# RWKV6 block in a fused hybrid layer: token differences made by TensorE, a second product for the decay's token, three mixing buffers, and a moved order of norms, copies and own terms

## The chip, the core and the metric

The kernel runs on one NeuronCore of a Trainium2 chip. The metric is the device time of one execution in microseconds, taken as the median of several executions. The profile is one further execution, seen by the hardware profiler. Its engines are PE (TensorE, matrix products), PEld (TensorE's weight loads), DVE (VectorE), ACT (ScalarE), POOL (GpSimd) and SP (SyncE, which here only starts transfers).

## The reference

The input `x` has 4 sequences of 1024 tokens with 256 channels, all in float32. Four sublayers are added to it one after another, each on a layer-normalised copy: a retention attention, a mixture of experts (8 experts, the best 2 for each token), an RWKV6 attention, and the same mixture of experts again. The change concerns the RWKV6 part:

```python
def _rwkv6_forward(x, time_maa_x, time_maa_wkvrg, tm_w1, tm_w2, time_decay, td_w1, td_w2, time_faaaa, Wr, Wk, Wv, Wg, Wo, ln_w, ln_b):
    Bb, Tt, Cc = x.shape
    sx = jnp.concatenate([jnp.zeros_like(x[:, :1]), x[:, :-1]], axis=1) - x
    xxx = x + sx * time_maa_x
    m = jnp.tanh(xxx @ tm_w1).reshape(Bb, Tt, 5, A)
    delta = jnp.einsum('btfa,fac->btfc', m, tm_w2)
    mix = time_maa_wkvrg[None, None] + delta
    xw, xk, xv, xr, xg = [x + sx * mix[:, :, i] for i in range(5)]
    r = xr @ Wr
    k = xk @ Wk
    v = xv @ Wv
    g = jax.nn.silu(xg @ Wg)
    ww = time_decay + jnp.tanh(xw @ td_w1) @ td_w2
    w = jnp.exp(-jnp.exp(ww))
    ...
    def step(state, rkvw):
        r_t, k_t, v_t, w_t = rkvw
        a = k_t[..., :, None] * v_t[..., None, :]
        y = jnp.einsum('bhk,bhkv->bhv', r_t, state + u[None, :, :, None] * a)
        new_state = w_t[..., :, None] * state + a
        return (new_state, y)
    ...
    yn = (y - mu) * jax.lax.rsqrt(var + EPS)
    yn = yn * ln_w.reshape(H, K) + ln_b.reshape(H, K)
    return yn.reshape(Bb, Tt, Cc) * g @ Wo
```

There are 16 heads of 16 channels (H, K), A is 32 and the decay's inner width is 64. `sx` is the difference between the token before and the token itself; the five mixed tokens `xw`, `xk`, `xv`, `xr`, `xg` are called mixing 0 to 4 below.

## The kernel before

**Stages.** The retention attention fills the first 285 us or so of the profiled execution. Two expert stages follow, for the two halves of the tokens; during the second one, the first block of the RWKV6 part is prepared in between (`prepare`, lists `first`). The RWKV6 stage runs from about 684 to 1303 us, and two more expert stages end the kernel. In the expert stages, tiles of 128 gathered tokens go through `fetch`, `up`, `turn` and `down`; `down` writes its result to a buffer `m_y` (L719, four buffers), which GpSimd scatters to DRAM (L720).

**The RWKV6 stage.** The tokens are cut into 8 blocks of 512 tokens, two per sequence; the loop at the end of `hybrid_kernel` goes over the blocks j and over 8 steps n in each. A step makes two `run` calls (h = 0 and 1), so that 16 calls cover the states of a block. One `run` multiplies v, broadcast from DRAM into `w_vb`, by k (L984, VectorE), scans it along time with the decay (L986, two scans) into `w_s`, and multiplies the states by r (L994, GpSimd). TensorE then adds the products over channels into `w_yp` (`sums`, L1017), one step later. `w_wk` holds the decay factor and k for one half of the channels (`factors`, L926 and L927, ScalarE); its two buffers are written once each per block.

**Beside the scans** each step does a part of the work for the next block j+1 and the rest of the work for the block before. The order of both is written out by hand: the tables `amid` (after the first `run` of a step), `late` (after the second), `uses` (small VectorE operations between two scans of a `run`) and `given` (which mixing products are made after which `run`). Each entry names the block relative to j. The engines TensorE, ScalarE, VectorE, GpSimd and, in this stage, the transfer queue of SyncE take their instructions strictly in the order in which these tables issue them.

**From tokens to the mixed tokens.** `normed` takes the statistics of a block (VectorE, then four small GpSimd operations), normalises into `w_xn` (L809, ScalarE, tokens on partitions) and puts the last column of the block before at the head of `w_xT`. `turn` transposes to `w_xT` (L212, L213; channels on partitions, 513 columns) and makes `w_sx`, the difference of neighbouring columns, on GpSimd (L825). `mix` makes the inner products of the token mix (L837, L840). `deltas` makes the five mixing products (L854), adds the constant part on ScalarE (L866), multiplies by `w_sx` (L867) and adds the token (L868), both on GpSimd; in blocks 6 and 7 mixings 0 and 2 take one VectorE operation (L864) in place of L866 and L867. The results lie in `w_xf`, four buffers. `decay` and `decay2` (L876, L887) make the decay from mixing 0, `projected` (L898) makes v, k, r and g from the others.

**From the states to the output.** The own term of a token is r times k (`paired`, L909, `w_rk`), summed over channels by TensorE (`own`, L915, `w_cp`) and multiplied by v (`bonus`, L920). `centre`, `spread`, `root`, `spread_out` and `gated` are the normalisation over heads; `out_part` (L220) is the output projection in two parts (0 and 2), and `added` puts them onto the residual (L225).

**PSUM.** Nearly all products share three buffers of one bank (`psum`, tag `mm`), so a product waits until the reader of an older one is done.

Of the kernel before, what the change touches and what calls it, by code (L numbers as in the profile page):

```python
# [42 lines left out]
P = 128  # L43
# [31 lines left out]
N_KEEP = O_PAD + NSL  # L75
# [28 lines left out]
def hybrid_kernel(  # L104
# [71 lines left out]
    dest = cst[:, O_DEST : O_DEST + HT]  # L176
    empty = cst[:, O_PAD : O_PAD + NSL]
# [287 lines left out]
    class Half:  # L465
# [245 lines left out]
        def down(self, j):  # L711
            op = psum([P, C], "m_op", "yp")
            for c in range(KC):
                mm(op, lhsT=self.aT[j][:, c, :],  # L714
                   rhs=w2a[:, bass.ds(self.ev[j], 1), c, :].rearrange("p o n -> p (o n)"),
                   start=(c == 0), stop=(c == KC - 1))
            g, i = divmod(j, GRP)
            y = px.tile([P, C], F32, name="m_y", tag="m_y", bufs=4)
            nc.scalar.activation(y, op, AF.Copy, scale=self.share[g][:, i : i + 1])  # L719
            nc.gpsimd.indirect_dma_start(  # L720
                out=y_views[self.half][j][:, :],
                out_offset=bass.IndirectOffsetOnAxis(ap=self.to[g][:, i : i + 1], axis=0),
                in_=y, in_offset=None,
            )
# [61 lines left out]
    def rwkv(pi, w):  # L786
# [13 lines left out]

        def normed(j):
            d = st[j]
            r = res[j]
            rstd = small.tile([P, NT], F32, name="w_rstd", tag="rstd")
            shift = small.tile([P, NT], F32, name="w_shift", tag="shift")
            stats_of(r, rstd, shift, "w_")
# [10 lines left out]
        def turn(j):  # L817
            d = st[j]
            xT = d["xT"]
            for n in range(2):  # L820
                across(lambda i: d["xn"][:, i, :], n,
                       xT[:, :, 1 + 2 * n * P : 1 + (2 * n + 2) * P], "w_")
            d["now"] = xT[:, :, 1 : BLK + 1]
            d["sx"] = full(pi, "w_sx", 1)
            nc.gpsimd.tensor_sub(d["sx"], xT[:, :, 0:BLK], d["now"])  # L825
# [18 lines left out]
        def deltas(j, parts):  # L844
# [12 lines left out]
            def mixed():  # L857
                for f, c, dp in dps:
                    if c == 0:
                        d["xf", f] = full(pi, "w_xf", 4)  # L860
# [7 lines left out]
                    nc.gpsimd.tensor_add(xf, xf, d["now"][:, c, :])  # L868
# [3 lines left out]
        def decay(j):  # L872
            d = st[j]
            tp = psum([P, BLK], "w_twp")
            for c in range(KC):
                mm(tp[:64, :], lhsT=w["td_w1"][:, c, :], rhs=d["xf", 0][:, c, :],  # L876
                   start=(c == 0), stop=(c == KC - 1))
# [197 lines left out]
        def out_part(j, i):  # L1075
            st[j]["op"] = project_part(st[j]["z"], w["o"], i, "w_")

        def added(j, i):
            add_part(st[j]["op"], res[j], i)

        def both(j, parts):
# [6 lines left out]
            [(0, normed)],  # L1088
            [(0, turn)],
# [3 lines left out]
            [(0, both, [(2, 0), (2, 1)]), (0, decay), (1, normed)],  # L1093
# [4 lines left out]
            [(1, turn)],  # L1098
# [12 lines left out]
            0: [(0, factors, 1), (1, mix, 0)],  # L1111
            1: [(0, own, 0), (0, projected, "g", 4)],
# [3 lines left out]
            5: [(1, decay2), (2, normed)],  # L1116
            6: [(1, projected, "k", 1)],
            7: [(-1, out_part, 2), (1, projected, "r", 3), (1, factors, 0)],
        }
        late = {  # L1120
            0: [],
            1: [(-1, centre, 1), (0, own, 1)],
# [4 lines left out]
            6: [(-1, out_part, 0)],  # L1127
            7: [(2, turn), (0, centre, 0)],
# [3 lines left out]
            (1, 0): [(0, paired, 1)],  # L1132
            (1, 1): [(0, bonus, 0)],
# [61 lines left out]
        def finish(n):  # L1195

            if n == 0:
                sums(NBLK - 1, 7)
# [5 lines left out]
    def rwkv_inputs(pi):  # L1204
# [17 lines left out]
        for n, src in (("v", w_v), ("g", w_g)):  # L1222
            t = pi.tile([P, KC, C], F32, name=f"w_{n}")
            flat = pi.tile([P, KC, C], F32, name=f"w_{n}0", tag="w_xf", bufs=4)
# [277 lines left out]
def constants():  # L1502
# [9 lines left out]
    c[:, O_NUM : O_NUM + NSL] = np.arange(NSL)  # L1512
    c[:, O_DEST : O_DEST + HT] = P * np.arange(HT) + i[:, None]
# [74 lines left out]
```

## Time and profile before

| | us |
|---|---|
| median of the shown runs | 1632.54 (1630.13 to 1636.39, 3 runs) |
| the profiled execution, own time | 1625.96 |
| its span | 1623.7 |
| busy PE, DVE, ACT, POOL | 1389.8, 989.4, 617.1, 937.0 |
| mean granted TensorE clock | 0.907 |

Of the RWKV6 stage alone, 684 to 1303 us: PE 504.6, DVE 553.0, ACT 243.1, POOL 544.6 us busy, clock 0.85. In the page's part 2 each digit is the busy share of a fortieth of the span in tenths. In a table of windows each row is a stretch of time with the busy time of every engine and, at the end, the granted TensorE clock as a share of full speed. In a row of groups stand the line, the engine, the operation, output and inputs, the count, the busy time, the mean duration in ns, and after the second bar the idle time of the engine before these instructions with what ended it. In a row of waits stand who waited for whom, the time in all, how often, and the longest. In a timeline row stand start, duration, engine, line, what is done, and in brackets the idle time before with its releaser. A float32 product shows as two records.

### The profile page before, as it was taken

To read this page: it belongs to the slowest core of one execution; us is meant where nothing else is said; L and a number is where in the kernel's file an instruction comes from. 1 tells how busy PE (TensorE), PEld (TensorE's weight loads), DVE (VectorE), ACT (ScalarE), POOL (GpSimd) and SP (SyncE) were. 2 spreads that over 40 slices of the span, in tenths; PEclk is the share of its full clock that TensorE was granted. 3 is DMA by queue.
4 is the path that set the end of the run, shared out by engine and by line. 5 is a ranking of instruction groups with operands and counts; after the bars stand their busy time and mean duration, and the time that the engine had idled before them with its cause. 6 is when DMAs were issued, how large, how long until landed. Compare 5 with 4: busy or idle time off the path is not lost.

```text
span 1623.7 us, 21398 instructions
## 1 busy us (share of the span) xinstructions
PE 1389.8 (86%) x6812; PEld 730.0 (45%) x6812; DVE 989.4 (61%) x1866; ACT 617.1 (38%) x1474; POOL 937.0 (58%) x895
## 2 busy tenths in 40 slices
PE   6999998868988899988879888897697679989993
PEld 4666665645555554522233333332232235555662
DVE  6566655423423532397979798989989824323534
ACT  2333434323443333444343444352344133443331
POOL 4233323723365345299999899976699832553331
PEclk9999998979999999998989799987788578999997
DMA  8931211232234431266655454533355921334625
GB/s 299 324 111 45 61 53 43 78 105 83 92 112 132 130 102 56 63 161 157 161 130 155 104 150 110 151 96 91 107 144 148 271 90 47 117 113 146 200 82 178
DMA packets 111595, 202.82 MB, mean 125 GB/s; under 512 B 12192, under 2 KB 73600, under 8 KB 111488
## 3 DMA queue, kind: packets, MB, share of 16 engines
q1 hardware_dynamic: 89280, 153.47, 33.1%
q0 software_dynamic: 17856, 41.70, 8.3%
q10 hardware_dynamic: 4352, 6.29, 1.3%
q8 instruction: 59, 0.97, 0.3%
q14 instruction: 48, 0.39, 0.1%
HBM read 140.96 MB, written 60.45 MB: 124 GB/s over the span
## 4 chain that ended last, share of the span: by engine, by line
PE 55%; POOL 18%; DVE 11%; issue 6%; ACT 6%; DMA 2%; another core or an unknown queue 0%; SPq 0%; ACTq 0%; POOLq 0%; DVEq 0%
PE m_hp L680 15%; POOL w_s L994 8%; PE m_op L714 7%; PE a_qkp L286 3%; PE w_pp L898 3%; DVE w_s L986 3%; POOL w_xf L867 3%; POOL w_xf L868 2%; PE a_yp L345 2%; PE m_xtp L671 2%; PE m_atp L707 2%; PE a_sp L325 2%; PE w_yp L1017 2%; PE w_dp L854 2%; PE a_op L220 2%
## 5 line engine op out<-in xcount | busy, mean ns | idle before, releaser
L720 POOL DMA_INDIRECT y_all<-m_y,m_to x156 | 150.9, 967 | 309.6 <-ACT m_xt L675 179.2
L994 POOL TENSOR_TENSOR w_s<-w_s,w_rT 128x1024 f32<-128x1024 f32 x128 | 304.1, 2417 | 34.0 <-DVE w_s L986 27.8
L680 PE MATMUL m_hp<-w1a,m_xt 128*128 x624 | 309.4, 620 | 12.5 <-ACT m_xt L675 12.3
L686 DVE TENSOR_TENSOR m_a<-m_hp,m_sg 128x256 f32<-128x256 f32 x156 | 66.1, 424 | 344.4 <-ACT m_sg L684 300.7
L714 PE MATMUL m_op<-w2a,m_aT 128*128 x624 | 165.1, 388 | 15.1 <-ACT m_y L719 10.8
L984 DVE TENSOR_TENSOR w_vb<-w_vb,w_wk 128x1024 f32<-128x1024 f32 x128 | 153.2, 1197 | 31.4 <-ACT w_wk L927 28.2
L986 DVE TENSOR_TENSOR_SCAN w_s<-w_wk,w_carry,w_vb 128x512 f32<-128x512 f32 x128 | 160.9, 1276 | 9.9 <-PE w_yp L1017 2.2
L986 DVE TENSOR_TENSOR_SCAN w_s<-w_wk,w_vb 128x512 f32<-128x512 f32 x128 | 152.7, 1215 | 15.4 <-ACT w_carry L1004 7.3
L680 PEld LDWEIGHTS m_hp<-w1a,m_xt 128*128 128x128 f32 x624 | 111.6, 199 | 94.4 <-issue 80.4
L652 POOL DMA_INDIRECT xg_all<-m_row,m_at x128 | 124.6, 973 | 45.9 <-issue 30.0
L1017 PE MATMUL w_yp<-w_s,core_c 128*32 128x512 f32 x512 | 104.8, 708 | 42.6 <-POOL w_s L994 32.0
L684 ACT ACTIVATE m_sg<-m_hp 128x256 f32<-128x256 f32 x156 | 60.1, 385 | 172.7 <-PE m_hp L680 141.0
L719 ACT ACTIVATE m_y<-m_op,m_share 128x256 f32<-128x256 f32 x156 | 74.0, 474 | 133.5 <-PE m_op L714 90.0
L714 PEld LDWEIGHTS m_op<-w2a,m_aT 128*128 128x128 f32 x624 | 107.5, 192 | 30.2 <-ACT m_y L719 17.0
L298 POOL TENSOR_TENSOR a_t<-a_t,a_t 128x512 f32<-128x512 f32 x32 | 41.1, 1285 | 119.1 <-DVE a_t L297 108.9
L867 POOL TENSOR_TENSOR w_xf<-w_xf,w_sx 128x512 f32<-128x512 f32 x72 | 94.0, 1306 | 24.1 <-ACT w_xf L866 23.0
L868 POOL TENSOR_TENSOR w_xf<-w_xf,w_xT 128x512 f32<-128x512 f32 x80 | 87.1, 1091 | 5.7
L707 PEld LDWEIGHTS m_atp<-cst,m_a 128*128 128x128 f32 x312 | 43.9, 144 | 93.7 <-issue 75.3
L328 DVE TENSOR_TENSOR a_pt<-a_sp,ret_c 128x2048 f32<-128x2048 f32 x32 | 73.1, 2285 | 15.8 <-PE a_sp L325 15.7
L675 ACT COPY m_xt<-m_xtp 128x256 f32<-128x256 f32 x156 | 57.1, 367 | 35.7 <-PE m_xtp L671 33.8
L671 PE MATMUL m_xtp<-cst,m_xg 128*128 128x128 f32 x312 | 62.5, 284 | 6.9 <-DMA m_xg<-xg_all 6.2
L709 DVE COPY m_aT<-m_atp 128x256 f32<-128x256 f32 x156 | 64.8, 415 | 5.4 <-PE m_xtp L671 2.6
(228 smaller groups left out, 2411.9 us busy)
## 6 DMA issues: line engine op xcount, KB each, us to landing
w_vb<-v_all SPq DMA_DIRECT2D x125, 512.0 KB
m_xg<-xg_all SPq DMA_DIRECT2D x36, 520.0 KB
tab<-in_rope SPq DMA_DIRECT2D x32, 512.0 KB
m_back<-y_all SPq DMA_DIRECT2D x48, 256.0 KB
xg_all<-zero SPq DMA_DIRECT2D x18, 520.0 KB
v_all<-w_vT SPq DMA_DIRECT2D x64, 128.0 KB
res<-in_x SPq DMA_DIRECT2D x8, 512.0 KB
w1a<-in_w SPq DMA_DIRECT2D x8, 512.0 KB
```

The costliest lines, as they stand in the source:

```text
L652: nc.gpsimd.indirect_dma_start(out=xg_views[self.half][2 * i + n][:, :], out_offset=bass.IndirectOffsetOnAxis(ap=self.at[n][:, i : i + 1], ...
L671: nc.tensor.transpose(tp[:, c, :], self.xg[j // GRP][:, j % GRP, c * P : (c + 1) * P], ident)
L680: mm(hp, lhsT=self.xt[j][:, c, :], rhs=w1a[:, bass.ds(self.ev[j], 1), c, :].rearrange("p o n -> p (o n)"), start=(c == 0), stop=(c == KC - 1))
L707: nc.tensor.transpose(tp[:, c, :], self.act[j][:, c * P : (c + 1) * P], ident)
L714: mm(op, lhsT=self.aT[j][:, c, :], rhs=w2a[:, bass.ds(self.ev[j], 1), c, :].rearrange("p o n -> p (o n)"), start=(c == 0), stop=(c == KC - 1))
L720: nc.gpsimd.indirect_dma_start(out=y_views[self.half][j][:, :], out_offset=bass.IndirectOffsetOnAxis(ap=self.to[g][:, i : i + 1], axis=0), ...
L867: nc.gpsimd.tensor_mul(xf, xf, sx)
L868: nc.gpsimd.tensor_add(xf, xf, d["now"][:, c, :])
L984: nc.vector.tensor_mul(vb, vb, wk[:, 1:2, :].to_broadcast([P, 2, BLK]))
L986: nc.vector.tensor_tensor_scan(s[:, q, 1 : BLK + 1], wk[:, 0, :], vb[:, q, :], 0.0 if j % NB == 0 else st[j - 1]["carry"][:, n, 2 * h + q ...
L994: nc.gpsimd.tensor_mul(s[:, :, 0:BLK], s[:, :, 0:BLK], d["r"][:, g, :].unsqueeze(1).to_broadcast([P, 2, BLK]),)
L1017: mm(d["yp", g][32 * q : 32 * q + 32, :], lhsT=w["sel"][:, i, :], rhs=d["s", n, q // 2][:, q % 2, 0:BLK], start=False, stop=(i == 3), skip ...
```

## The change

- The constants get a 128x128 matrix `lag` with -1 on the diagonal and +1 above it. A new function `lagged` makes `w_sx` on TensorE: for each of the four token tiles and both channel halves one product of `w_xn` with `lag`, and, but for the first tile, a one-column product that adds the last token of the tile before. ScalarE copies the result to `w_sx` in two copies. For the second block of a sequence GpSimd adds the head column of `w_xT` to the first column. The GpSimd difference in `turn` is gone.
- For mixing 0 the token is no longer added on GpSimd; `decay` makes two more products, of `td_w1` with the token itself, in the same sum.
- `w_xf` has three buffers, `m_y` six.
- `normed` is split into `norms` (statistics) and `normed` (normalisation and head column).
- In the steps: the statistics stay in step 5 and the normalisation goes to step 6; `turn` goes from step 7 to step 6, `lagged` stands at the end of step 7; output part 0 goes from late to amid in step 6, part 2 from amid in step 7 to late in step 6, each with a PSUM handle of its own; `factors` 0 of the next block goes ahead of the r projection in step 7; `centre` 0 goes from the end of step 7 to the middle of the next step 0; `own` 0 goes to the end of step 0, `own` 1 to the middle of step 1; `paired` 1 goes from step 1 to step 0 and `bonus` 0 from the second to the first `run` of step 1.

```diff
@@ hybrid_kernel, constants
+    lag = cst[:, O_LAG : O_LAG + P]
@@ Half.down
-            y = px.tile([P, C], F32, name="m_y", tag="m_y", bufs=4)
+            y = px.tile([P, C], F32, name="m_y", tag="m_y", bufs=6)
@@ rwkv
-        def normed(j):
-            d = st[j]
-            r = res[j]
+        def norms(j):
+            d = st[j]
             rstd = small.tile([P, NT], F32, name="w_rstd", tag="rstd")
             shift = small.tile([P, NT], F32, name="w_shift", tag="shift")
-            stats_of(r, rstd, shift, "w_")
+            stats_of(res[j], rstd, shift, "w_")
+            d["norm"] = rstd, shift
+
+        def normed(j):
+            d = st[j]
+            r = res[j]
+            rstd, shift = d["norm"]
             xn = d["xn"] = pi.tile([P, NT, C], F32, name="w_xn", tag="w_xn", bufs=1)
...
             d["now"] = xT[:, :, 1 : BLK + 1]
-            d["sx"] = full(pi, "w_sx", 1)
-            nc.gpsimd.tensor_sub(d["sx"], xT[:, :, 0:BLK], d["now"])
+
+        def lagged(j):
+
+            d = st[j]
+            xT = d["xT"]
+            sx = d["sx"] = full(pi, "w_sx", 1)
+            for n in range(2):
+                lp = psum([P, 2 * KC, P], "w_lp").rearrange("p (i k) t -> p i k t", k=KC)
+                for i in range(2):
+                    t = 2 * n + i
+                    for k in range(KC):
+                        cols = slice(k * P, (k + 1) * P)
+                        mm(lp[:, i, k, :], lhsT=d["xn"][:, t, cols], rhs=lag, start=True,
+                           stop=(t == 0))
+                        if t > 0:
+                            mm(lp[:, i, k, 0:1], lhsT=d["xn"][96:P, t - 1, cols],
+                               rhs=ident[96:P, P - 1 : P], start=False, stop=True)
+                nc.scalar.copy(
+                    sx[:, :, 2 * n * P : (2 * n + 2) * P].rearrange("p k (i t) -> p i k t", i=2),
+                    lp)
+            if j % NB > 0:
+                nc.gpsimd.tensor_add(sx[:, :, 0:1], sx[:, :, 0:1], xT[:, :, 0:1])
...
-                        d["xf", f] = full(pi, "w_xf", 4)
+                        d["xf", f] = full(pi, "w_xf", 3)
...
-                    nc.gpsimd.tensor_add(xf, xf, d["now"][:, c, :])
+                    if f > 0:
+                        nc.gpsimd.tensor_add(xf, xf, d["now"][:, c, :])
...
         def decay(j):
             d = st[j]
             tp = psum([P, BLK], "w_twp")
-            for c in range(KC):
-                mm(tp[:64, :], lhsT=w["td_w1"][:, c, :], rhs=d["xf", 0][:, c, :],
-                   start=(c == 0), stop=(c == KC - 1))
+            for n, z in enumerate((d["now"], d["xf", 0])):
+                for c in range(KC):
+                    mm(tp[:64, :], lhsT=w["td_w1"][:, c, :], rhs=z[:, c, :],
+                       start=(n + c == 0), stop=(n + c == KC))
...
         first = [
-            [(0, normed)],
-            [(0, turn)],
+            [(0, norms), (0, normed)],
+            [(0, turn), (0, lagged)],
...
-            [(1, turn)],
+            [(1, turn), (1, lagged)],
...
         amid = {
-            0: [(0, factors, 1), (1, mix, 0)],
-            1: [(0, own, 0), (0, projected, "g", 4)],
+            0: [(0, factors, 1), (1, mix, 0), (-1, centre, 0)],
+            1: [(0, own, 1), (0, projected, "g", 4)],
             2: [(1, mix, 1)],
             3: [(1, projected, "v", 2)],
             4: [(-1, spread_out, 0), (1, decay)],
-            5: [(1, decay2), (2, normed)],
-            6: [(1, projected, "k", 1)],
-            7: [(-1, out_part, 2), (1, projected, "r", 3), (1, factors, 0)],
+            5: [(1, decay2), (2, norms)],
+            6: [(2, normed), (1, projected, "k", 1), (-1, out_part, 0)],
+            7: [(1, factors, 0), (1, projected, "r", 3)],
         }
         late = {
-            0: [],
-            1: [(-1, centre, 1), (0, own, 1)],
+            0: [(0, own, 0)],
+            1: [(-1, centre, 1)],
             2: [(-1, spread)],
             3: [],
             4: [(-1, spread_out, 1)],
             5: [(1, store)],
-            6: [(-1, out_part, 0)],
-            7: [(2, turn), (0, centre, 0)],
+            6: [(2, turn), (-1, out_part, 2)],
+            7: [(2, lagged)],
         }
         uses = {
             (0, 0): [(0, paired, 0)],
-            (1, 0): [(0, paired, 1)],
-            (1, 1): [(0, bonus, 0)],
+            (0, 1): [(0, paired, 1)],
+            (1, 0): [(0, bonus, 0)],
             (2, 0): [(0, bonus, 1)],
...
         def finish(n):
 
             if n == 0:
+                centre(NBLK - 1, 0)
                 sums(NBLK - 1, 7)
@@ constants
+    c[:, O_LAG : O_LAG + P] = np.eye(P, k=1) - np.eye(P)
```

More of the change, by code (lines that the diff above doesn't have):

```diff
@@ L74 @@
 O_PAD = O_DEST + HT
-N_KEEP = O_PAD + NSL
+O_LAG = O_PAD + NSL
+N_KEEP = O_LAG + P
 O_CAUSAL = 0
@@ L798, in full @@
             return where.tile([P, KC, n], F32, name=name, tag=name, bufs=bufs)
+        def norms(j):
+            d = st[j]
+            rstd = small.tile([P, NT], F32, name="w_rstd", tag="rstd")
+            shift = small.tile([P, NT], F32, name="w_shift", tag="shift")
+            stats_of(res[j], rstd, shift, "w_")
+            d["norm"] = rstd, shift
         def normed(j):
@@ L803, in normed @@
             r = res[j]
-            rstd = small.tile([P, NT], F32, name="w_rstd", tag="rstd")
-            shift = small.tile([P, NT], F32, name="w_shift", tag="shift")
-            stats_of(r, rstd, shift, "w_")
+            rstd, shift = d["norm"]
             xn = d["xn"] = pi.tile([P, NT, C], F32, name="w_xn", tag="w_xn", bufs=1)
@@ L1075, in out_part @@
         def out_part(j, i):
-            st[j]["op"] = project_part(st[j]["z"], w["o"], i, "w_")
+            st[j]["op", i] = project_part(st[j]["z"], w["o"], i, "w_")
         def added(j, i):
-            add_part(st[j]["op"], res[j], i)
+            add_part(st[j]["op", i], res[j], i)
         def both(j, parts):
@@ L1092, in rwkv @@
             [(0, both, [(1, 0), (1, 1)])],
-            [(0, both, [(2, 0), (2, 1)]), (0, decay), (1, normed)],
+            [(0, both, [(2, 0), (2, 1)]), (0, decay), (1, norms), (1, normed)],
             [(0, both, [(3, 0), (3, 1)])],
@@ L1223, in rwkv_inputs @@
             t = pi.tile([P, KC, C], F32, name=f"w_{n}")
-            flat = pi.tile([P, KC, C], F32, name=f"w_{n}0", tag="w_xf", bufs=4)
+            flat = pi.tile([P, KC, C], F32, name=f"w_{n}0", tag="w_xf", bufs=3)
             nc.sync.dma_start(out=flat, in_=src.rearrange("(k p) n -> p k n", p=P))
```

## The prediction

> **What bounds the kernel now.** I read the page's 40 slices first, to see which engine is full where.
>
> ```profile
> PE   6999998868988899988879888897697679989993
> ...
> DVE  6566655423423532397979798989989824323534
> ...
> POOL 4233323723365345299999899976699832553331
> ```
>
> A slice is 40.6 us. In slices 18 to 32 VectorE and GpSimd are full together and TensorE is not: that is the RWKV stage (TensorE's own slices there are mostly 7 to 9). Before and after it lie the expert stages, where TensorE is full. The chain that ended last agrees: inside the stage it runs over GpSimd's products `w_s` (L994), the mixing products (L867, L868) and VectorE's scans (L986). So I cut the stage at each block's first `w_vb` product on VectorE; three of the eight blocks:
>
> ```profile
> core 0: us, PE busy (x) PEld busy (x) DVE busy (x) ACT busy (x) POOL busy (x), PEclk, DMA share, GB/s
> ...
> 755.50:828.50 73.00, 60.77 (x207) 21.23 (x206) 67.84 (x79) 30.10 (x66) 71.65 (x48) 0.93 0.65 155
> 828.50:907.00 78.50, 68.35 (x232) 24.91 (x232) 66.30 (x79) 32.45 (x64) 72.70 (x67) 0.87 0.57 141
> 907.00:983.00 76.00, 66.16 (x233) 24.60 (x232) 68.13 (x79) 33.16 (x72) 68.17 (x48) 0.89 0.44 122
> ```
>
> VectorE has about 68 us of work per block, GpSimd 68 to 73, and a block takes 73 to 78.5. Neither is full alone: each waits for the other, through TensorE and ScalarE. What VectorE, which drives the recurrence, waits for in the whole stage:
>
> ```profile
> DVE w_vb L984 <- ACT w_wk L927: 28.2, 7, 15.9
> DVE w_bonus L920 <- PE w_cp L915: 11.6, 7, 2.5
> DVE w_s L986 <- ACT w_carry L1004: 7.3, 2, 6.2
> ```
>
> The 15.9 us is the entry into the stage; the rest of the first row, 12.3 us, is some 2.4 us at the end of most blocks. All its waits after the entry come to 47 us (these three rows without the 15.9 give 31.2). Last, the timeline at the end of block 2 shows where they come from:
>
> ```profile
> 892.46 2.08 ACT L809 ACTIVATE w_xn<-res,w_shift,w_rstd 128x256 f32<-128x256 f32 x4 [11.78 <-POOL w_xT L813]
> ...
> 894.82 1.92 PE L1017 MATMUL w_yp<-w_s,core_c 128*32 128x512 f32 x4 [3.20 <-POOL w_s L973]
> 896.67 3.78 PE L220 MATMUL w_op<-w_o,w_sq 128*128 128x256 f32 x8
> 900.25 2.33 PE L898 MATMUL w_pp<-w_xf,w_r 128*128 128x512 f32 x4
> ...
> 907.01 1.22 DVE L984 TENSOR_TENSOR w_vb<-w_vb,w_wk 128x1024 f32<-128x1024 f32 x1 [2.58 <-ACT w_wk L927]
> ...
> 923.24 1.12 PE L915 MATMUL w_cp<-w_rk,w_sum 128*128 128x512 f32 x2
> ...
> 924.40 0.69 DVE L920 TENSOR_TENSOR w_bonus<-w_cp,w_vT 128x512 f32<-128x512 f32 x1 [1.59 <-PE w_cp L915]
> ```
>
> TensorE stands still until GpSimd delivers `w_s` (894.8), and then owes everything at once: output part 2, the r projection, mixing product 4, the turn, the centring, another sum, the token mix, and only then the own term `w_cp` (923.2). The decay factors `w_wk` queue on ScalarE behind the r copies of that chain.
>
> **The change, part by part.**
>
> GpSimd loses work. Prices:
>
> ```profile
> L868 POOL TENSOR_TENSOR w_xf<-w_xf,w_xT 128x512 f32<-128x512 f32 x72 | 78.3, 1091 | 5.0
> ...
> L825 POOL TENSOR_TENSOR w_sx<-w_xT 128x1024 f32<-128x1024 f32 x7 | 13.3, 1894 | 3.8 <-ACT w_xT L213 3.8
> ```
>
> Per block one difference (1.89) and the two additions of mixing 0 (2 x 1.09): 4.07 us, seven times 28.5 us. Added: four 2-column additions, some 0.2 us each by the 2-column copy L815 (186 ns). This is no direct gain; it lowers the lower bound of a block on GpSimd (length less its idle time over 0.25 us) from 72.7, 74.2, 69.4 to 68.6, 70.1, 65.3 in the three blocks shown, near or below VectorE's (70.4, 68.5, 70.6).
>
> TensorE gains work: per block 8 products of 128x128 and 6 one-column corner products (8 less the 2 of the first token tile), each in two passes, 28 records; and for the decay two more products, 4 records. Nearest rows: L512, also 128 weight columns with few moving columns, and L876 itself.
>
> ```profile
> 868.52 1.95 PE L512 MATMUL m_lp<-wr,m_tT 128*128 128x8 f32 x16
> ...
> 618.47 1.93 PE L876 MATMUL w_twp<-w_xf,w_td_w 128*64 128x512 f32 x4
> ```
>
> The next record begins 1.81 us after the first (0.113 each) and 1.87 us after the second. So 28 x 0.113 + 1.87 = 5.0 us per block at full clock. The Trainium skill (TensorE: Matmul & The Clock Gate, Back-to-back issue gap) gives N/2.4 + 2.5 ns, or some 25 ns for the smallest: 16 x 56 + 12 x 25 + 4 x 216 ns = 2.1 us. The row is twice that and this kernel's own float32, so I take 5.0. In the RWKV stage TensorE idles 10 to 12 us per block, which covers it; without cover it is 5 us per block. But the preparation of block 0 lies in the second expert stage, which TensorE bounds (163 of 176 us busy): there all 5.0 us count. Block 1's difference, 3.2 us, falls just after the entry, into a block with 13 us of TensorE gaps: nothing, at most 3.2.
>
> ScalarE gains two copies per block (L213's price, 0.59 each). It is 40% busy: no throughput cost. But they bring a wait: `w_sx` has one buffer, so the copy follows GpSimd's last multiplication by the old one, and TensorE's difference products, and behind it on ScalarE stand the second `w_wk` pair and so VectorE's second `w_rk`, which the change also moves ahead, from step 1 to step 0. In block 3 GpSimd ends that multiplication near 911.8, 4.8 us after VectorE began the block; two copies and the pair take 2.4 us more: 7.2. VectorE asks after two vb products, three scans and one `w_rk`, about 6.9 us.
>
> Moves. `factors` goes ahead of the r copies: the pair that ended at 906.98 can run behind the k copies, near 897, and the 2.4 us stop at block ends goes: -12.3. The statistics stay in step 5 while the four normalisations go to step 6, which gives GpSimd half a step more before ScalarE stops for it; the 6.2 us in block 0 came through such a stop (ScalarE's carry copy was late): -6.2. The own terms go ahead of a sum and of mixing products, so the old `w_cp` waits go: -11.6.
>
> What is late next is the same chain. Output parts 0 and 2 and the turn now stand before the sum, but the turn needs the normalisation, which ends 2.1 us after GpSimd's statistics (892.4 to 894.5), then two k copies and a turn copy, then output part 2 and the sum: r begins 8 to 10 us after the statistics, as now (900.25). From r to the own term, by the rows of this boundary, partly at half clock: r 5.7, mixing 4.6, difference 3.2 with 1.3 for its copy, sum 1.9, token mix 4.2, centring 1.8, own term 0.5: 23.2 us; with passes at full clock about 17. VectorE, if it begins at 904.4 (907.0 less the 2.58), asks for the own term 11.1 us into the block, 23 us after the statistics. GpSimd ran those statistics 9 us after VectorE had them ready (890.6 against 881.7); 4 us less work bring it some 4 us nearer, so VectorE asks at 27, and the own term comes between 25 and 33. Together with the `w_rk` wait that is 0 to 6 us at each block start; no trace row shows it. I take 1.5, near the full-clock end because the moved turn and output part fill idle time of TensorE: +10.5 at seven starts.
>
> The `w_xT` edge copy goes behind two `w_s` products, and nobody needs it before the next block. No DMA is added or changes its place on SP's or GpSimd's queue against its neighbours; the sends and joins there only have less ahead of them.
>
> Three mixing buffers: each reuse falls behind a projection that TensorE does before the product that fills the buffer, so zero; if not, mixing waits for one projection (3.6 us). Six `m_y` buffers: before L719 ScalarE waited 3.6 us in all for what the profile calls remote, which I read as the scatter of an older `m_y`: -2, between 0 and -3.6. The first constant load grows by 64 KB, at the first slice's 299 GB/s 0.2 us: +0.3 with its start.
>
> Sum: -12.3 - 11.6 - 6.2 + 10.5 + 5 - 2 + 0.3 = -16.3 us, on the profiled execution's 1625.96 (span 1623.7 and 2.3 around it). That execution lies 6.6 below the shown median 1632.54, so against the median: 1632.5 - 16.3 = 1616.2.
>
> **The rivals.**
>
> (a) VectorE becomes the sole bound. Its lower bounds per block sum to 572 us of the stage's 618.5. If the remaining 47 us of waits nearly vanish, -47 + 5 - 2 = -44: 1588. For: GpSimd's bounds fall to about VectorE's. Against: before, the larger of the two bounds per block summed to 589, and the stage still took 29 more; two full engines that feed each other don't run without waits.
>
> (b) The waits are exchanged: `w_wk`, `w_cp` and the carry go (-30), the block starts cost 3.5 each (+25), the entry 5, `m_y` -2: -2, 1630. For: the own term's arrival, 25 to 33, straddles the 27. Against: nothing but the clock.
>
> (c) Slower: TensorE's chain at the block boundary takes GpSimd's place. It is in order, and after 3.2 us of idling the four records at 894.8 took 1.92 us where 1.05 is usual; by block the granted clock is 0.71 to 0.93. The skill's page (Part 1: The HAM clock gate) gives half rate after one idle window of about 3.4 us until a busy window has passed; by it alone the chain, once its gaps are filled, would take 17 us and cost nothing; by the rows it takes 23.2 with 5 us of new work behind waits of its own. At the late end 6 us at each of seven starts: 42 - 30.1 + 5 - 2 = +15, 1647. It decides from about 4 us per start, r to own term above some 22 us.
>
> **How the numbers follow.** Half a per cent, 8 us, is about what a measurement of this kernel can tell from no change. The main case (-28 to -9) has 0.47, (a) 0.13, (b) 0.20, (c) 0.20. (b) splits into 0.03 faster, 0.15 same, 0.02 slower, (c) into 0.02 same and 0.18 slower: faster 0.63, same 0.17, slower 0.20. The range runs from (a)'s value almost to (c)'s, leaving out what lies beyond: 1588 to 1645.
>
> **What would show it.** Right: blocks 2 to 4 at about 72 us; the `w_wk` row of VectorE's waits near its entry alone, `w_cp` near zero; GpSimd's difference row gone and its addition at 64 in place of 80; new short stops of `w_rk` for ScalarE; the second expert stage longer by 5. Wrong: blocks still at 76 with `w_cp` waits or a long `w_rk` wait, a lower clock at the boundary (c), or no wait left on VectorE at all (a).

## The result, and the profile after

The changed kernel took 1680.49 us (median of 4 runs, 1677.47 to 1682.40) beside 1633.60 for the kernel before in the same runs (1630.13 to 1636.39): a ratio of 1.0302, with a 95% interval of 1.0271 to 1.0334. It is 47 us slower, where 16 us faster was forecast, and it lies outside the range. The profiled execution has a span of 1677.1 us against 1623.7.

Where the 53.4 us of span lie follows from three times: the first expert product `m_hp`, VectorE's first `w_vb` of block 0, and its first `w_vb` of block 7. The first came 7.3 us later (357.2, now 364.5), in code that the change doesn't touch. In the traces of the experiments that place lies anywhere from 347 to 366 us, with and without the new constants, so I read nothing into it. From there to block 0 it was 6.1 us more (5.0 were forecast for the expert stage), over the first seven blocks 41.2 us (547.9, now 589.1), and in the rest 1.2 us less. The loss is in the RWKV blocks.

The slices of VectorE, GpSimd and TensorE's granted clock:

```profile
PEclk9999998879999999998879797978788778999997
...
DVE  6576556423523432398958686869998943423534
...
POOL 3233323633465244399968686867488962564331
```

Where VectorE and GpSimd had been full together, both now dip to 5 and 6 tenths in every second slice, about once per block. The same three blocks as before the change, in the windows view:

```profile
core 0: us, PE busy (x) PEld busy (x) DVE busy (x) ACT busy (x) POOL busy (x), PEclk, DMA share, GB/s
768.15:845.54 77.39, 67.99 (x243) 26.59 (x241) 68.06 (x79) 31.55 (x69) 70.46 (x46) 0.89 0.60 146
845.54:933.26 87.72, 75.30 (x265) 32.90 (x266) 66.32 (x80) 34.12 (x67) 68.94 (x66) 0.84 0.51 125
933.26:1020.50 87.24, 75.83 (x264) 32.75 (x262) 68.22 (x80) 34.16 (x74) 64.08 (x46) 0.82 0.40 110
```

VectorE's work is unchanged, GpSimd's is 1 to 4 us less, and the blocks are 4 to 11 us longer. What grew is TensorE: 7 to 10 us per block, at a lower clock. VectorE's waits in the stage (engine, line, what it waited for: us, times, longest):

```profile
DVE w_rk L938 <- ACT w_wk L956: 51.4, 7, 11.4
DVE w_vb L1013 <- ACT w_wk L956: 15.9, 1, 15.9
DVE w_bonus L949 <- PE w_cp L944: 9.5, 5, 3.0
DVE w_varp L1082 <- ACT q_y L1074: 8.3, 3, 4.0
```

The `w_wk` wait at `w_vb` is down to the stage's entry, as forecast, and the carry wait is gone. In their place stands the second `w_rk`, 51.4 us in seven waits. The longest one in the timeline, at the start of block 2 (845.54):

```profile
843.38 2.06 PE L927 MATMUL w_pp<-w_xf,w_r 128*128 128x512 f32 x4
...
850.68 2.07 PE L881 MATMUL w_dp<-w_m,tm_w2b 32*128 32x512 f32 x2 [0.78 <-ACT w_xf L893]
...
853.52 1.65 PE L843 MATMUL w_lp<-cst,w_xn 128*128 128x128 f32 x6 [0.78 <-ACT w_xf L893]
...
861.30 0.58 PE L846 MATMUL w_lp<-cst,w_xn 32*128 32x1 f32 x2
...
861.92 0.58 ACT L848 COPY w_sx<-w_lp 128x512 f32<-128x512 f32 x1 [4.32 <-PE w_lp L846]
862.40 0.61 ACT L955 ACTIVATE w_wk<-w_ew 128x512 f32<-128x512 f32 x1
...
863.66 0.69 DVE L938 TENSOR_TENSOR w_rk<-w_wk,w_rT 128x512 f32<-128x512 f32 x1 [11.39 <-ACT w_wk L956]
```

r, then mixing product 4, then the 28 records of the difference from 853.5 to 861.9, then ScalarE's second copy, then the second pair of decay factors, and only then VectorE. The difference took 8.4 us. The windows view of these microseconds says why; the column behind POOL is the granted clock:

```profile
853.50:861.90 8.40, 8.38 (x32) 6.94 (x36) 0.00 (x0) 0.58 (x1) 6.40 (x10) 0.50 0.01 2
861.90:864.00 2.10, 2.10 (x9) 0.44 (x10) 0.34 (x1) 1.68 (x3) 0.18 (x1) 0.50 0.00 0
864.00:866.00 2.00, 2.00 (x3) 0.85 (x3) 2.00 (x3) 0.00 (x0) 0.44 (x1) 0.50 0.00 0
866.00:868.00 2.00, 2.00 (x4) 0.82 (x3) 1.82 (x2) 0.00 (x0) 2.00 (x4) 0.63 0.62 176
868.00:870.00 2.00, 2.00 (x6) 0.82 (x5) 0.00 (x0) 0.60 (x1) 1.29 (x1) 1.00 0.40 87
```

TensorE is busy without a break from 853.5 on, and its clock stays at half until about 867.5 (0.63 is the mean of half and full over the row from 866 to 868). At four of the seven block starts the set took 7.7 to 8.4 us like this one, at three, at 0.95 to 1.00 of the clock, 4.9 to 5.0: 46.9 us in all, near the 41.2 us that the first seven blocks lost. These blocks as a whole, before the change and after it:

```profile
684.48:1232.40 547.92, 456.60 (x1535) 164.46 (x1533) 487.82 (x577) 217.08 (x453) 480.19 (x394) 0.87 0.51 132
697.93:1287.03 589.10, 499.55 (x1758) 207.10 (x1757) 488.29 (x577) 224.51 (x467) 450.74 (x376) 0.85 0.47 122
```

TensorE is busy for 43.0 us more, and its idle time stayed what it was: 91.3 us before, 89.6 after.

### The profile page after: what moved, and what is told of

The parts are those of the page before. It is cut to its first block, busy times and chain, and to the rows that moved or that the text cites. A ratio compares the mean times of both kernels' runs of the same rounds, so it can differ in the third digit from the quotient of the medians.

```text
span 1677.1 us, 21924 instructions
## 1 busy us (share of the span) xinstructions
PE 1438.5 (86%) x7068; PEld 779.5 (46%) x7068; DVE 988.9 (59%) x1866; ACT 624.3 (37%) x1490; POOL 905.5 (54%) x875
## 4 chain that ended last, share of the span: by engine, by line
PE 62%; DVE 13%; POOL 10%; ACT 6%; issue 5%; DMA 2%; another core or an unknown queue 1%; SPq 0%; DVEq 0%; POOLq 0%; ACTq 0%
PE m_hp L682 15%; PE m_op L716 7%; DVE w_s L1015 5%; POOL w_s L1023 4%; PE w_pp L927 4%; PE a_qkp L288 3%; PE m_atp L709 3%; PE a_yp L347 2%; DVE w_vb L1013 2%; PE w_dp L881 2%; PE w_yp L1046 2%; PE m_xtp L673 2%; PE a_sp L327 2%; PE w_mp L864 2%; PE w_lp L843 2%
## 5 line engine op out<-in xcount | busy, mean ns | idle before, releaser
L682 PE MATMUL m_hp<-w1a,m_xt 128*128 x624 | 304.9, 612 | 11.0 <-ACT m_xt L677 10.9
L1046 PE MATMUL w_yp<-w_s,core_c 128*32 128x512 f32 x512 | 92.1, 706 | 20.0 <-POOL w_s L1023 20.0
L896 POOL TENSOR_TENSOR w_xf<-w_xf,w_xT 128x512 f32<-128x512 f32 x64 | 69.8, 1091 | 4.7
L222 PE MATMUL w_op<-w_o,w_sq 128*128 128x256 f32 x128 | 47.9, 534 | 23.3 <-ACT w_xT L215 13.6
```

The lines of the kernel that those rows point to most:

```text
L682: mm(hp, lhsT=self.xt[j][:, c, :], rhs=w1a[:, bass.ds(self.ev[j], 1), c, :].rearrange("p o n -> p (o n)"), start=(c == 0), stop=(c == KC - 1))
L1046: mm(d["yp", g][32 * q : 32 * q + 32, :], lhsT=w["sel"][:, i, :], rhs=d["s", n, q // 2][:, q % 2, 0:BLK], start=False, stop=(i == 3), skip ...
```

## The experiments

Theory: the time of the difference on TensorE is the loss. It can act as a place in ScalarE's queue (the pair of factors stands behind its copies) or as TensorE's own time. Rival: the new order is at fault. The experiments ran in several batches, in which the kernel before takes from 1596 to 1632 us; so only ratios to the kernel before in the same batch are compared.

**Another place, behind the decay factors (lag_behind_factors).**

```
-  0: [(0, factors, 1), (1, mix, 0), (-1, centre, 0)],      7: [(2, lagged)],
+  0: [(0, factors, 1), (1, lagged), (1, mix, 0), (-1, centre, 0)],      7: [],
```

> The changed kernel with one call moved: the token differences of the next block (TensorE's products and ScalarE's two copies) are issued in step 0 behind the second pair of decay factors, in place of the end of step 7 ahead of it. Theory (the pair stands behind the two copies on ScalarE, so VectorE's second w_rk waited 51.4 us in seven blocks): that wait falls below 10 us and the time to about 1642 (1632 to 1652), while TensorE's products of the difference stay as slow as they are. Rival (TensorE's additional work at the block boundary is the bound, whoever stands behind it): the time stays at 1668 to 1682, and the wait turns up again at the own term w_cp, at w_vb or at GpSimd's products.

Ratio 1.0278 (1.0228 to 1.0328), the rival's number. VectorE's waits:

```profile
DVE w_bonus L949 <- PE w_cp L944: 49.8, 6, 11.1
...
DVE w_rk L938 <- ACT w_wk L956: 10.9, 6, 7.5
```

The wait changed its name, from the second factors to the own term, and kept its length. ScalarE's queue was only where it showed. This theory fell. (The preparation already makes block 1's difference, and here it is made a second time, 28 records more; the first block takes 79.6 us, 70.2 in the changed kernel. By that length the ratio is up to 0.6 points too high, and still far above the theory's.)

**The difference on GpSimd, all else changed (sub_on_gpsimd).** The body of `lagged` becomes one line:

```
+ nc.gpsimd.tensor_sub(d["sx"], d["xT"][:, :, 0:BLK], d["now"])
```

> The changed kernel with its whole new order, but the token difference again one GpSimd subtraction, in the place where the changed kernel has TensorE's products. Theory (the difference by TensorE with its copies is what costs, the new order does not): the second w_rk waits under 15 us in all, and the time is about 1622 (1608 to 1636), 5 us of it from the second expert stage. Rival (the new order is at fault: norms later, own terms earlier, output parts before the turn): 1660 or more, with waits on w_rk or w_cp of 30 us or more.

Ratio 0.9929 (0.9909 to 0.9949): faster than before. The rest of the change is worth 0.7%, the difference on TensorE costs 3.7 points on top.

**The difference on TensorE, nearly nothing else changed (before_lag3).** `lagged` behind the turn in the kernel before, with three mixing buffers for room.

> The kernel before with the difference by TensorE right behind the turn and three mixing buffers in place of four (for the room that the constant matrix needs); nothing else of the change. Theory: the old order puts the turn and the difference ahead of the second pair of decay factors too, so the second w_rk waits 35 to 60 us and the time is 1660 to 1685. Rival (the order of the change is at fault): no more than 1645.

Ratio 1.0301 (1.0263 to 1.0340). With the last one this settles it: the difference costs about 3% in the old order and 3.7 points in the new one, so the order isn't at fault. (The three mixing buffers don't explain it: sub_old_decay below has them too, in the new order, and is as fast as the kernel before.) The time is what I expected, the place is not: the second `w_rk` has no wait of any size here, and the longest new waits stand at four scans, 18.4 us for decay factors and 17.6 us for a `w_s` buffer that the sums had not read.

**TensorE's time alone (tensor_time_alone).** The products stay, their copies go, GpSimd subtracts.

> The changed kernel with the difference again by one GpSimd subtraction, while TensorE still runs all 28 records of the difference's products in their place at the block boundary; nothing reads them, ScalarE's copies of them and GpSimd's edge addition are left out. Theory (TensorE's time at the boundary is the whole price, one for one, since the chain to the own term runs through it): within 8 us of the changed kernel, a ratio of 1.022 to 1.034 to the kernel before, with the wait on the own term w_cp at 35 us or more. Rival (the price is the way through ScalarE's copies and the waits on them): within 10 us of the kernel with the subtraction alone, a ratio of 0.990 to 1.000.

Ratio 1.0314 (1.0252 to 1.0375), as slow as the whole change, though nothing reads the products. Its waits:

```profile
DVE w_bonus L945 <- PE w_cp L940: 25.8, 6, 6.0
DVE w_s L1011 <- PE w_yp L1042: 23.7, 5, 6.3
...
DVE w_rk L934 <- ACT w_wk L952: 12.0, 6, 6.5
```

Half of it stands at the own term, half at scans that wait for a `w_s` buffer which the sums on TensorE have not yet read: one late engine under two names. The wait on `w_cp` that I expected at 35 us was 25.8; the time is what was expected.

**Fewer records: the first columns by GpSimd (edges_on_gpsimd).**

```
-  if t > 0: mm(lp[:, i, k, 0:1], lhsT=d["xn"][96:P, t - 1, cols], rhs=ident[96:P, P - 1 : P], ...)
-  nc.gpsimd.tensor_add(sx[:, :, 0:1], sx[:, :, 0:1], xT[:, :, 0:1])
+  edge = sx.rearrange("p k (t q) -> p k t q", q=P)[:, :, :, 0]
+  nc.gpsimd.tensor_add(edge, edge, xT[:, :, 0:BLK].rearrange("p k (t q) -> p k t q", q=P)[:, :, :, 0])
```

> The changed kernel without the six one-column products of the difference; the first column of each token tile is put right by one GpSimd addition over four columns of each channel half, where the changed kernel adds one. Theory: at the boundaries with half the clock the products took 8.3 us, 3.5 of it (6 x 0.58) by the one-column products, at full clock 4.8 and 2.3; that much less stands ahead of the second pair of decay factors at seven boundaries, so 16 to 24 us are regained: 1656 to 1665. Rival (the order is at fault): within 4 us of the changed kernel, 1676 to 1684.

Ratio 1.0096 (1.0063 to 1.0130), a larger gain than expected: 2.06 points, some 33 us, by leaving out 12 records of 28.

**The same records in another order (edges_last).** The one-column products behind the four full products of their half.

> The changed kernel with the one-column products of the difference behind the four full products of their half in place of between them; same records, same place at the block boundary. Theory A (what made them dear, 2.8 us at full clock for 12 records, is the change between products over 128 rows and products over 32 rows, 11 times per block): the set of 28 records takes about 3.4 us at full clock in place of 4.87, and the ratio to the kernel before falls from 1.030 to about 1.020. Theory B (a one-column record is dear wherever it stands): the set stays at 4.6 us or more and the ratio at 1.027 to 1.032.

Ratio 1.0231 (1.0177 to 1.0284): theory A. The set at full clock, in TensorE's timeline (start, duration of the group, records at the end of the line):

```profile
772.61 1.16 PE L841 MATMUL w_lp<-cst,w_xn 128*128 128x128 f32 x8
773.70 0.60 PE L845 MATMUL w_lp<-cst,w_xn 32*128 32x1 f32 x4
774.23 1.16 PE L841 MATMUL w_lp<-cst,w_xn 128*128 128x128 f32 x8
775.31 1.05 PE L845 MATMUL w_lp<-cst,w_xn 32*128 32x1 f32 x8
```

From start to start a record takes 0.136 us (1.09 for 8), with 128 columns, and 0.133 with one (0.53 for 4). In the changed kernel, where they alternate, two records with 128 columns take 0.42 and two with one column 0.31 (774.07 to 774.49 to 774.80 in its timeline at the start of block 1). The change between the two kinds makes 3.75 us into 4.87 at full clock; at 0.55 of the clock, 6.3 us (edges_last, from 1020.5) stand beside 7.7 (changed kernel, from 1027.1).

The four kernels with a `lagged` in this place form a series. The sets at the seven block starts, added up from their timelines, and the ratio:

| kernel | sets, us | ratio |
|---|---|---|
| sub_on_gpsimd | 0 | 0.9929 |
| edges_on_gpsimd | 20.2 | 1.0096 |
| edges_last | 36.6 | 1.0231 |
| changed kernel | 46.9 | 1.0302 |

A microsecond of these products costs about 1.3 us of time (3.73 points of 1633.60 us are 61 us for 46.9; 1.67 are 27 for 20.2). The set in the second expert stage, 4.8 us in the changed kernel, is a part of the surplus, since the sum does not hold it. Another part is the clock of the products around: over the first seven blocks TensorE is busy for 499.6 us in the changed kernel and 442.6 in sub_on_gpsimd, 57.0 us more for 46.9 us of sets, at a mean clock of 0.85 and 0.89; the blocks are 52.4 us longer.

**Behind both own terms (lag_behind_own, lag_behind_own_edges).** Both own terms in the late part of step 0, the difference behind them; the second one without the one-column products.

> The changed kernel with the difference behind both own terms, in the late part of step 0 (the second own term comes forward from step 1, with a product of its own for each half), ahead of the first use of the difference in step 1. Same 28 records. If the price is that they stand in the chain from the r projection to the own terms, the wait on w_cp is under 15 us and the ratio 0.990 to 1.008. If TensorE has no room for them in the blocks' first half wherever they stand, the wait moves on, to the mixing products, the centring and GpSimd's products, and the ratio stays at 1.020 to 1.032.

> The last one with the token tiles' first columns put right by one GpSimd addition in place of the one-column products: 16 records, 2.05 us at full clock and 3.7 at half. If the chain is what counts, 0.983 to 0.993, since GpSimd also sheds the subtraction (1.9 us per block); if TensorE has no room there, about 1.010, as with the same difference at the old place (1.0096).

Ratios 1.0322 (1.0287 to 1.0356) and 1.0082 (1.0049 to 1.0114): as at the old place. (Both make block 1's difference twice too, 28 and 16 records more.) The waits of the first:

```profile
DVE w_varp L1082 <- ACT q_y L1074: 18.7, 4, 5.1
...
DVE w_xf L891 <- PE w_dp L881: 18.5, 4, 8.0
DVE w_s L1015 <- PE w_yp L1046: 17.6, 7, 4.4
```

The own term's wait is down to 3.9 us, and the next things that TensorE delivers, directly or through ScalarE, are late instead. The sets themselves ran at 0.91 to 1.00 of the clock at five of the six starts after block 1's, yet the mean over the first seven blocks is 0.85 as in the changed kernel: other products ran at half the clock in their place. No place among those tried was free. (In the new order, a place right behind the turn wasn't tried; there GpSimd still reads the only `w_sx` buffer for the block before.)

**What the other parts are worth (sub_old_decay, sub_four_y, decay_alone, order_alone).**

> The kernel with the subtraction on GpSimd, and the decay as before: GpSimd adds the token to mixing product 0 and TensorE makes two products in place of four. If two more products on TensorE cost what GpSimd's two additions (2.2 us per block) bring, it is within 3 us of the kernel with the subtraction (ratio 0.993). If TensorE's second product is part of the price (1.87 us in the second expert stage, 1.9 to 3.7 in each block), it is faster, 0.984 to 0.990. If GpSimd's load is the bound, slower, 0.998 to 1.004.

> The kernel with the subtraction on GpSimd, with four m_y buffers as before in place of six. By the prediction's term the six buffers are worth 2 us (0 to 3.6), so this is at a ratio of 0.993 to 0.9965; if they are worth nothing, at 0.993 like the kernel with six; if they set the pace of the scatters, at 0.998 or more.

> The kernel before with the decay's change alone: GpSimd no longer adds the token to mixing product 0, TensorE makes four products in place of two. With the subtraction on GpSimd this part was worth 0.7% (0.9999 without it, 0.993 with it). If it brings the same in the old order (GpSimd's load is what paces the blocks), 0.991 to 0.996; if it needs the new order, 0.998 to 1.002; by the prediction's step (1.87 us more in the second expert stage, no direct gain) 1.001.

> The kernel before with the new order alone (norms, decay factors, own terms, output parts, turn), four mixing buffers, the old decay and the old constants. By the prediction's steps (12.3, 11.6 and 6.2 us of waits gone, 10.5 come) about 20 us faster: 0.988. If the three mixing buffers ate the gain of the order in the kernel with the old decay (0.9999), 0.988 to 0.995 as well. If the waits only change places while GpSimd's load paces the blocks, 0.998 to 1.003.

| kernel | ratio (95%) |
|---|---|
| kernel before, new order alone | 0.9990 (0.9970 to 1.0009) |
| kernel before, decay alone | 0.9986 (0.9968 to 1.0004) |
| sub_old_decay: all but decay and difference | 0.9999 (0.9974 to 1.0023) |
| sub_four_y: order, three mixing buffers, decay | 0.9932 (0.9913 to 0.9952) |
| sub_on_gpsimd: that and six `m_y` | 0.9929 (0.9909 to 0.9949) |

Neither the order nor the decay gains anything alone that can be measured; together they bring 0.7%. The `m_y` buffers bring nothing. Why the order alone brings nothing stands in its waits:

```profile
DVE res L225 <- PE w_op L220: 24.3, 7, 7.1
DVE w_vb L992 <- ACT w_wk L935: 19.3, 2, 15.9
DVE w_bonus L928 <- PE w_cp L923: 6.6, 4, 1.9
```

The waits at `w_vb` and `w_cp` shrank, and VectorE waits for the output parts instead, 24.3 us where it was 7.6. The output part behind the turn is late at least in part because the turn's copies are: with the edge copy early, below, this wait falls from 18.6 us (sub_on_gpsimd) to 12.5 (sub_edge_early).

**A wait that the move had made (sub_edge_early, sub_edge_k, after_edge_k).** In the changed kernel ScalarE's waits have these rows:

```profile
ACT w_xT L215 <- POOL w_xT L822: 15.4, 3, 11.0
ACT w_xT L215 <- POOL w_xT L820: 5.4, 3, 1.8
```

The copies of the turn write the same `w_xT` tile as GpSimd's edge copy and wait for it, and that one now stands behind `w_s` products; one wait of 11.0 us, at the end of block 5, is half of the sum. In these three kernels it goes back to the statistics in step 5; in two of them the k copies also go ahead of the normalisations:

```
   def norms(j): ...
+      xT = d["xT"] = ...; the memset or edge copy of xT[:, :, 0:1]
-  6: [(2, normed), (1, projected, "k", 1), (-1, out_part, 0)],
+  6: [(1, projected, "k", 1), (2, normed), (-1, out_part, 0)],
```

> The kernel with the subtraction on GpSimd, and the edge copy of w_xT back at the statistics. Theory (the same chain ends last here): 2.9 us at each of seven boundaries, less what other waits take back: a ratio of 0.978 to 0.988 to the kernel before (0.993 without this). Rival (GpSimd's load paces the blocks): 0.990 to 0.996.

> The last one with the k projection's copies ahead of the normalisations too: by the theory 1.2 us more at each boundary, 0.973 to 0.985; by the rival as the last one. If ScalarE's wait for the k projection holds up the normalisations, it is slower than the last one by 5 us or more.

> The changed kernel with GpSimd's copy of w_xT's edge column back at the statistics (step 5), and the k projection's copies ahead of the four normalisations on ScalarE. Theory (ScalarE's turn copies wait 2.9 us for the edge copy behind w_s products, the turn another 1.2 us for the k copies, and both lie in the chain at the block's start): 15 to 28 us faster than the changed kernel, a ratio of 1.013 to 1.021. Rival (that chain is not what ends last): 1.027 to 1.033.

With the subtraction on GpSimd 0.9885 (0.9852 to 0.9918) and 0.9867 (0.9839 to 0.9895); with the difference on TensorE 1.0212 (1.0183 to 1.0241), 0.9 points or some 15 us better than the change. In sub_edge_early the two rows are replaced by one:

```profile
ACT w_xT L215 <- PE w_xtp L214: 6.4, 11, 1.9
```

All three fall just short of the expected ranges. The edge copy alone brings 0.4 points on sub_on_gpsimd, with intervals that overlap a little, and the second step's 0.2 points lie within the intervals; the two steps together are clear of noise, 0.6 points there and 0.9 on the change.

**Half the clock (gap_filled).** The changed kernel with eight needless products where TensorE idled ahead of the turn:

```
-  st[j]["op", i] = project_part(st[j]["z"], w["o"], i, "w_")
+  st[j]["op", i] = project_part(st[j]["z"], w["o"], i, "w_", 8 if i == 0 else 0)   # 8 more products into op first
```

> The changed kernel with eight further 512-column products on TensorE ahead of output part 0 (3.4 us at full clock; output part 0 overwrites what they write), where TensorE idled 5.2 us before the turn. If half the clock is what made the difference dear and an idle stretch is what lowers it, the sets of 28 records after it take about 4.9 us in place of 8.3 at the boundaries of blocks 2 to 5, the chain behind the turn shortens by some 8 us at each of them, and the ratio is 1.005 to 1.020. If the clock does not follow this idle stretch, the sets stay at 8.3 us and the ratio at 1.028 to 1.045.

Ratio 1.0074 (1.0051 to 1.0097): 2.3 points better by more work. The products took twice what I had reckoned, as each shows as two records (16 in 7.03 us):

```profile
807.67 7.03 PE L221 MATMUL w_op<-w_sq,cst 128*128 128x512 f32 x16
814.54 1.89 PE L225 MATMUL w_op<-w_o,w_sq 128*128 128x256 f32 x8
...
824.10 3.70 PE L930 MATMUL w_pp<-w_xf,w_r 128*128 128x512 f32 x8
...
830.51 0.38 PE L849 MATMUL w_lp<-cst,w_xn 32*128 32x1 f32 x2
...
834.63 0.58 PE L849 MATMUL w_lp<-cst,w_xn 32*128 32x1 f32 x2
```

The r projection, which had run in two halves of about 2 us with a stop between, takes 3.70 in one. The time is as expected; the sets at the starts of blocks 2 to 5 were to take about 4.9 us and took 4.9 to 7.3. All seven add up to 40.6 us (46.9 in the changed kernel), so most of the 2.3 points came from the products around them. Over the first seven blocks the mean clock is 0.92 (0.85 in the changed kernel); TensorE is busy for 510.8 us, 42.3 of them with needless products, so the others take 31.0 us less than the 499.6 there; the blocks are 33.2 us shorter. Within the set shown the clock falls again: a pair of one-column records takes 0.38 us at 830.5 and 0.58 at 834.6, with no idle time in between.

**What is left when all is put right (sub_edge_k_filled, after_mended).** Both have four needless products, the edge copy early and the k copies ahead. The first subtracts on GpSimd; after_mended makes the difference on TensorE, with the first columns on GpSimd.

> The kernel with the subtraction on GpSimd, the edge copy early and the k copies ahead (0.987), with four further 512-column products on TensorE ahead of output part 0 (3.5 us at full clock, against 1.9 us of idling there). If half the clock at the boundary costs this kernel too, the r projection and what follows run at full clock and the ratio is 0.970 to 0.982. If VectorE and GpSimd now pace the blocks, the products bring nothing or cost their surplus: 0.985 to 0.997.

> The changed kernel with the difference on TensorE and all that was found: one GpSimd addition for the four first columns in place of the one-column products, the edge copy early, the k copies ahead, four further products ahead of output part 0. If the difference pays where the clock holds (2.1 us on TensorE against 1.7 us off GpSimd), within 0.5% of the kernel with the subtraction and the same filling. If its time on TensorE is paid one for one even at full clock, some 2 to 3 us for each of seven boundaries and 2 us in the expert stage more: 1.0 to 1.5% above it.

0.9850 (0.9816 to 0.9885) and 0.9887 (0.9854 to 0.9919). The first is no better than sub_edge_k without the products, within the intervals. The clock of these two, sub_edge_k first:

```profile
PEclk9999999978999999999989989997788688999997
...
PEclk9999899978899999999999999997889688999997
```

It was nearly full in the RWKV blocks without the products (a mean of 0.90 over the first seven, 0.91 with them). There was little half clock left to fill, so what it still costs this kernel is not shown. After_mended beats the kernel before by 1.1%, and lies 0.4 points behind the first one, with overlapping intervals: inside the 0.5 that I had given it if the difference pays, but on the losing side. Its sets of 16 records took 2.0 to 2.1 us at full clock at four of the seven starts, 3.0 to 3.8 at the others. So the difference on TensorE shows no gain here, and no clear loss.

## Why the prediction was wrong

**Where the forecast broke: "TensorE idles 10 to 12 us per block, which covers it".** The 28 records were priced at 3.2 us. Against TensorE's load they were then set at nothing, and in the chain from r to the own term they stood with 3.2 us, of which hardly any reached the sum. Price and cover both failed. The price was that of records of one kind in a row (0.113 each, at L512); the difference alternates two kinds, and the set took 4.9 us at full clock and 7.7 to 8.4 near half. The formula that the prediction set beside it, 2.1 us, is in the Trainium skill (TensorE: Matmul & The Clock Gate, Back-to-back issue gap) that of an isolated product; it entered no sum. The cover was idle time in which TensorE waited in the very chain that the difference stands in: over the first seven blocks it came out as 89.6 us where it had been 91.3, with 43.0 us more of work. Idle time ahead of late input can't take work that comes after that input. The kernels with the set in three places, and the one with its products read by nobody, showed its time paid in full.

**The new wait, +10.5, with the mechanism right and the size wrong.** The text names it: copies of `w_sx` on ScalarE, behind them the second factors and the second `w_rk`, and in the other branch the own term. It took 1.5 us per start; the second `w_rk` and the own term now wait 60.9 us, 8.7 per start. r to own term was put at 23.2 us as recorded or 17 at full clock, and I chose near 17 "because the moved turn and output part fill idle time". In block 2 it is 26.6 us from the first r product (843.38) to the own term's (869.94).

**Rival (c) is what happened, and its point of decision was right:** more than 4 us per start. Its own price, 1647, was 33 us too low: 19 us are the block starts (60.9 us for its 42), since it held the difference at 3.2 us too, and some 12 are other waits for TensorE's chain that it left out (`w_varp` 8.3 us for 1.0 before, `w_cen` 7.6 for 2.9). A chance of 0.20 was too little, given that the half clock stood in the trace, and that the work was added to TensorE in just that chain.

**The clock rule.** I set the page's rule, half rate until a busy window of about 3.4 us has passed (the Trainium skill, TensorE: Matmul & The Clock Gate, Part 1: The HAM clock gate), against the recorded 23.2 us, and leant towards the rule. Here TensorE was recorded busy for 8.4 us at 0.50, and got its full clock only at about 867.5, 3.8 us after the 512-column products of the token mix had begun (863.7). As far as these traces show, the difference's narrow products did not count as the activity that lifts the clock; that they are too narrow is my reading, and no run here varied the width alone.

**The removed waits, -12.3, -11.6, -6.2.** The first and the third went as said. The own terms' went from 11.6 only to 9.5 in the changed kernel. But order_alone, which has all three moves without the difference, gains nothing that can be measured: rival (b), waits exchanged, was right for this part. What came late next was the output part, not the own term as I said.

**The edge copy: "nobody needs it before the next block".** Wrong. ScalarE's copies into the same tile waited for it, 20.8 us in all, and taking that away was worth some 0.4 points with the subtraction on GpSimd (0.9929 to 0.9885, with intervals that overlap a little).

**"This is no direct gain" for what GpSimd sheds, and +1.87 for the decay.** In the old order that fits (0.9986, about none). In the new one the decay's part is worth 0.7 points (0.9999 without it, 0.9932 with it); that GpSimd's 2.2 us per block count once the order's waits are out of the way is my reading. My sum had added parts that only work together.

**Small terms.** The `m_y` buffers are worth nothing (-2 was said, 0 lay in its range). The second expert stage and entry came to +6.1 for +5.0.

## What to carry to other kernels

Before work is moved to an engine because it has idle time, look at which side of its late input the new work falls: behind it, in a chain that ends last, it costs its full time, at the clock of that place and not the best one. Price a set of small products as it will be issued, alternations included, and not from a row of equal ones. And when waits are removed one by one, expect the next one to take their place until the engine that paces the block sheds work too: here order and decay gained only together.

## What the hardware showed that I had not expected

- More work made the kernel faster: eight needless products per block, 7 us each time, took 2.3 points off. The mean clock over the first seven blocks rose from 0.85 to 0.92, and TensorE's other products took 31.0 us less.
- A fully busy TensorE stayed at half the clock for 8.4 us of 128-column and one-column float32 products, and in gap_filled its clock fell from full to half within such a set (0.38, then 0.58 us for a pair of one-column records) without idle time.
- Alternating between products over 128 rows with 128 columns and products over 32 rows with one column made 28 records 1.1 us longer at full clock (4.87 against 3.75 us).
